# Transposing x from the fifth block on: 32x32 squares on VectorE and DMAs within SBUF in place of TensorE

## The chip, the cores and the metric

The kernel runs on one core of a Trainium2 chip. The metric is the device time of one execution in microseconds (us). The engines are called as the profile calls them: PE (TensorE; PEld is its weight load), DVE (VectorE), ACT (ScalarE), POOL (GpSimd) and SP (SyncE, which here only issues DMAs). A "q" behind an engine's name is its queue of instructions that issue DMAs or wait.

## The reference

The input x has 8 x 1024 tokens of 256 channels, fp32. A linear-attention layer with 16 heads of 16 channels is followed by a feed-forward layer with ternary weights; each is added to its input and normalised.

```python
q, k, v = x @ Wq.T + bq, x @ Wk.T + bk, x @ Wv.T + bv      # split into 16 heads
q = softmax(q, axis=-1)                                    # over the 16 channels of a head
k = softmax(k, axis=-2)                                    # over the 1024 tokens of a batch
out = einsum('bhnd,bhde->bhne', q, einsum('bhnd,bhne->bhde', k, v))
x = layernorm(x + (layernorm(out) * ln_g + ln_b) @ Wo.T + bo)
h = gelu((layernorm(x) * ln1_g + ln1_b) @ ternary(w1).T + b1)
x = layernorm(x + (layernorm(h) * ln2_g + ln2_b) @ ternary(w2).T + b2)
```

## The kernel before

The 8192 tokens are cut into 16 blocks of 512, two to a batch. A block's x is one SBUF tile of 128 partitions x 4 x 256: partition p holds four of the block's tokens (t = 0 to 3). For the projections x is needed with channels on partitions: xT is a tile of 128 x 2 x 512, one half of 128 channels for each k, with the 512 tokens in its columns. `turn_x` makes it. For each k, `turned` has PE transpose four squares of 128x128 into one PSUM bank (L341, the tile ptx) and ACT copies the bank to xT (L342). `turned` also turns the queries after their softmax (`turn_queries`, the tile ptq, copied to qT).

From xT, `queries` computes q (PE at L408, tile pq, stationary xT; DVE adds the bias at L412) with tokens on partitions, and `keys` computes the keys (PE at L362, tile pk) with channels on partitions and tokens in columns. `keys_exp` takes their exponential on ACT, with the sum over the tokens (L382, to ekT). `turn_keys` turns ekT back to tokens on partitions (PE at L395, ACT at L399), and `keys_x` multiplies with x (PE at L451, tile pa). `attend` applies the state of a whole batch to qT (PE at L546, tile po; ACT copies at L551 and L552; DVE's statistics sto at L556). `turn_input` turns the normalised input of the feed-forward layer (PE L633, ACT L637 and DVE L638 make the upper and the lower half of hT). `hidden` (PE L661, tile ph; ACT L667, L670, L651), `lower` (DVE L688, tile u) and `product` (PE L733, tile pf) are the feed-forward layer. `rest` closes a block on DVE (L805, L810, L814, L816). `finish` scales it on POOL (L847), stores it from SP (L850) and then loads the block nine further on into the same x tile (L77). The reductions of squares are DMAs on POOL's queue that accumulate within SBUF (sums from sq, L696; sums from sums, L704); two more add constant rows to x (L619 and L1000).

The order of the work is written out by hand. Each engine runs its instructions in the order of the program. The table ORDER has one string of pieces per slot: slots 0 to 3 use "early", slots 4 to 15 "mid", and five more close the work. In slot i the queries and keys of block i are computed, x of block i+1 is turned (tx0 and tx1, one for each k), and the feed-forward layer of a block some slots back runs in pieces (H, A, B). `m4` and the like pull steps of `rest` and of the norms from a list. In "mid", tx0 and tx1 stand 18 pieces apart, with the turned queries, two or three pieces of `attend` and the turned keys between them, and the first reader of the turned x is q0 of the next slot:

```python
"mid": """
    H m6 H m q0 q2 m1 m2 m3 m st0/tp qm m6 H st1/tp sq/w H p m k0 p k1 p kb p m3 H H A m8
    A A st2/w m1 H A tq0/tp H m3 A st3/w A ke p tx0 A bs m m4 m2 a/ph A m4 m a/w tq1/ph
    a/w te0 p B te2/w be qe p tx1/w p B B m1 en B bw qs x0 ti1/ph p m4 m a/w x1 m4 B cr
    m1 m3 ti0/ph B m2 m3 B m m2 p p B sh
"""
```

SP's queue holds the loads of the weights and of the first nine blocks at the start, and after that only one store and one load per finished block, 43 DMAs in all. Of the DMAs from SP and ACT, each waits in the built program for the one eight before it.

Of the kernel before, what the change touches and what calls it, by code (L numbers as in the profile page):

```python
# [8 lines left out]
F32 = mybir.dt.float32  # L9
I32 = mybir.dt.int32  # L10
F32R = mybir.dt.float32r
AF = mybir.ActivationFunctionType
# [3 lines left out]
P = 128  # L16
EPS = 1e-5
XBUFS = 9
BANKS = {"tp": 1, "w": 3, "ph": 2, "pf": 2}
LAG = 6  # L20
RING = 10
ROUND = 12582912.0

# [2 lines left out]
def attn_ffn_postln_kernel(  # L26
# [11 lines left out]
    nc = tc.nc  # L38
    B, N, C = x.shape
# [3 lines left out]
    KC = C // P  # L43
    HC = HID // P
    NT = N // P
    G = 4
# [3 lines left out]
    const = ctx.enter_context(tc.tile_pool(name="const", bufs=1))  # L50
    xpool = ctx.enter_context(tc.tile_pool(name="xpool", bufs=XBUFS))
    small = ctx.enter_context(tc.tile_pool(name="small", bufs=4))
    big = ctx.enter_context(tc.tile_pool(name="big", bufs=1))
# [1 line left out]


    wqkv_sb = const.tile([P, KC, 3 * C], F32, name="wqkv_sb")
    wo_sb = const.tile([P, KC, C], F32, name="wo_sb")

    t1 = const.tile([P, KC, HID], F32R, name="t1")  # L60

# [75 lines left out]
    def power(v, name):  # L137
# [5 lines left out]
        nc.gpsimd.tensor_tensor(y, v, mhalf[:, :n], ALU.pow)  # L143
        yield LAG
        nc.vector.tensor_tensor(t, y, y, ALU.mult)
# [15 lines left out]
    w1s, w2s = (  # L161
        [big.tile([P, 2 * TB], F32, tag="u", bufs=RING, name=f"{name}_{i}") for i in range(2)]
        for name in ("w1", "w2")
# [14 lines left out]
    def quantise(parts, t_sb, inv, name):  # L178
        part = small.tile([P, 2], F32, tag="part", name=f"part_{name}")
        for i, w in enumerate(parts):  # L180
            yield
            size = big.tile([P, 2 * TB], F32, tag="u", bufs=RING, name=f"size_{name}_{i}")
            nc.scalar.activation(size, w, AF.Abs, accum_out=part[:, i : i + 1])
# [26 lines left out]
    def rows_of(w, vecs, n, m, name):  # L210
# [3 lines left out]
        for j in range(n):  # L214
            nc.tensor.matmul(pr[:rows, :C], vecs(j), w(j), start=(j == 0), stop=(j == n - 1))
        row = big.tile([P, TB], F32, tag="u", bufs=RING, name=f"row_{name}")[:rows, :C]
        nc.vector.tensor_copy(row, pr[:rows, :C])
# [9 lines left out]
    def prepare1():  # L227
# [5 lines left out]
        nc.vector.tensor_scalar(gs1, ln1_g, inv1, None, ALU.mult)  # L233
        row = big.tile([P, 2 * TB], F32, tag="u", bufs=RING, name="row_1")[:2, :]
        for c in range(0, HID, TB):
# [85 lines left out]
    xT, q, qT, ekT, ek, pa = {}, {}, {}, {}, {}, {}  # L321
    es, mb, z, mx, a0, aT, sT, sm = {}, {}, {}, {}, {}, {}, {}, {}
    ys, mvo = {}, {}

    def x_of(i):
        return xs[i]
# [7 lines left out]
    def bank(name):  # L334
        return bank_of([P, TB], name)

    def turned(dst, src, k, name):

        pt = bank(name)
        for t in range(G):  # L340
            nc.tensor.transpose(pt[:, t * P : (t + 1) * P], src[:, t, k * P : (k + 1) * P], ident)  # L341
        nc.scalar.copy(dst, pt)  # L342

    def turn_x(i, k):
        if i >= len(blocks):
            return
        if k == 0:
            xT[i] = big.tile([P, KC, TB], F32, tag="xT", bufs=2, name=f"xT_{i}")
        turned(xT[i][:, k, :], x_of(i), k, f"ptx_{i}_{k}")

    def keys(i, c):

# [24 lines left out]
    def keys_exp(i):  # L377

        b, g = blocks[i]
        dst = big.tile([P, KC, TB], F32, tag="ekT", name=f"ekT_{i}")  # L380
        for c in range(KC):
            nc.scalar.activation(  # L382
                dst[:, c, :], ekT[i][c], AF.Exp, bias=mx[i][:, c : c + 1],
                accum_out=z[b][:, g, c : c + 1],
            )
        ekT[i] = dst

# [51 lines left out]
    def turn_queries(i, k):  # L439
        if not 0 <= i < len(blocks):  # L440
            return
        if k == 0:
            qT[i] = big.tile([P, KC, TB], F32, tag="qT", bufs=2, name=f"qT_{i}")
        turned(qT[i][:, k, :], q[i], k, f"ptq_{i}_{k}")

    def keys_x(i, c):

# [205 lines left out]
    def hidden(n):  # L653
# [13 lines left out]
        nc.scalar.activation(ph[n], ph[n], AF.Gelu, bias=bh[:, j : j + 1])  # L667
        u[n] = big.tile([P, 2, TB], F32R, tag="u", bufs=RING, name=f"u_{n}")
        if not upper_on_vector(n):
# [28 lines left out]
    def upper_on_vector(n):  # L698

        return len(blocks) - 4 < n // HC < len(blocks) - 1 and n % 3 == 1  # L700
# [244 lines left out]
    def piece(what, i):  # L945
# [33 lines left out]
        elif what == "kb" and real:  # L979
            keys_bias(i)  # L980
        elif what == "ke" and real:
            keys_exp(i)
        elif what == "bs" and real and g == 1:
            blocks_sum(b)
# [8 lines left out]
        elif what == "cr" and real:  # L993
# [8 lines left out]
            )  # L1002
        elif what in ("tx0", "tx1"):
            turn_x(i + 1, int(what[2]))
        elif what[:2] == "tq" and i > 0:
            one = turn("tq", NBL, KC)
            if one:
                turn_queries(*one)
# [37 lines left out]
        elif what == "sq" and i > 4:  # L1046
            one = turn("sq", NBL)
            if one:
# [3 lines left out]
                if n < NBL - 1:  # L1052
                    assert count["B"] >= (n + 1) * HC
                    behind.append([rest(n, (0, G)), 0])

    turn_x(0, 0)
    turn_x(0, 1)
    for i in range(last + 5):
        names = {last + k: str(16 + k) for k in range(5)}
        for what in ORDER[names.get(i, "early" if i < 4 else "mid")].split():  # L1060
            what, _, tag = what.partition("/")
# [48 lines left out]
```

## Time and profile before

| | |
|---|---|
| median of 3 runs | 669.87 us (665.34 to 671.02) |
| profiled execution | 667.08 us, of which the span of its instructions is 665.4 us |
| granted TensorE clock, mean | 0.974 |
| transposes of x (ptx) | 128 on PE; 32 copies to xT on ACT |
| DMA packets, bytes | 33889, 64.73 MB |
| share of 16 DMA engines: POOL's queue, SP's and ACT's queue | 39.8%, 7.9% |

The profile gives for each engine its busy time as a share of the span. The chain that ended last follows the work back from the last instruction, at each step to what released it, and divides the span among the engines and lines it passes. A group is all instructions of one line, operation and pair of tiles, with its busy time and the idle time just before them. A timeline row gives start, duration, engine, line, operation and tiles. A DMA row gives the time from its issue to its landing. The slots 6 to 14, from 190 to 521 us, take 36 to 37 us each; the tx0 and tx1 of the twelve blocks from the fifth on lie in slots 3 to 14. A slot is called odd or even by its number.

### The profile page before, as it was taken

The page shows a single profiled execution, that of the slowest core. Times are in us where ns is not written, and L with a number is a line of the kernel's source. Part 1 is how long each engine was busy: PE and PEld are TensorE (multiplying, and loading weights), DVE is VectorE, ACT ScalarE, POOL GpSimd, SP SyncE. Part 2 cuts the span into 40 slices and gives each one's busy share as a digit, 9 for nine tenths or more (in the row PEclk, how much of TensorE's full clock was granted, in tenths as well). Part 3 has the DMA queues.
Part 4 walks back from the last instruction along what each step waited for, and adds up shares of the span by engine and source line. Part 5 has one row for each costly group of instructions (what it writes and reads, how often), then busy time and mean ns, then how long its engine had stood idle before and what let it go on. Part 6 is the DMA issues. An engine that isn't in the chain of part 4 may idle for free.

```text
span 665.4 us, 9546 instructions
## 1 busy us (share of the span) xinstructions
PE 605.4 (91%) x3200; PEld 478.2 (72%) x3200; DVE 511.3 (77%) x1448; ACT 498.3 (75%) x939; POOL 338.6 (51%) x315
## 2 busy tenths in 40 slices
PE   5799989999999999999999999999999989778850
PEld 3467657878787787868787887878787777566750
DVE  1666776388877797888978887888878888867886
ACT  2554388798897979787887979797979887758720
POOL 1123453545464645646455646456464644765461
PEclk9999999999999999999999999999999999978875
DMA  8522232545365563637463755635354644372321
GB/s 289 208 33 33 32 49 47 96 80 96 48 159 80 115 122 83 129 67 151 80 149 59 159 79 119 120 82 103 61 121 75 125 75 107 56 119 70 89 63 64
DMA packets 33889, 64.73 MB, mean 97 GB/s; under 512 B 3344, under 2 KB 21776, under 8 KB 33840
## 3 DMA queue, kind: packets, MB, share of 16 engines
q0 software_dynamic: 25328, 43.92, 39.8%
q1 hardware_dynamic: 8240, 19.94, 7.9%
q8 instruction: 25, 0.41, 0.3%
q10 hardware_dynamic: 272, 0.26, 0.1%
q14 instruction: 24, 0.20, 0.1%
HBM read 11.95 MB, written 8.39 MB: 31 GB/s over the span
## 4 chain that ended last, share of the span: by engine, by line
PE 64%; DVE 12%; ACT 10%; DMA 4%; issue 4%; POOL 4%; SPq 1%; POOLq 0%; DVEq 0%
PE ph L661 13%; PE pf L733 11%; PE po L546 9%; PE pk L362 8%; PE pa L451 7%; PE pq L408 6%; DVE u L688 3%; ACT sq L651 2%; ACT ph L667 2%; DMA sums<-sums 2%; PE pth L633 2%; PE ptq L341 1%; PE pte L395 1%; PE ptx L341 1%; DVE x L805 1%
## 5 line engine op out<-in xcount | busy, mean ns | idle before, releaser
L733 PE MATMUL pf<-t,u 128*128 128x258 f32 x1024 | 164.0, 300 | 2.3 <-DVE u L688 1.3
L661 PE MATMUL ph<-hT,t 128*128 128x512 f32 x512 | 149.7, 423 | 13.3 <-DVE u L688 10.0
L733 PEld LDWEIGHTS pf<-t,u 128*128 128x128 f32 x1024 | 141.7, 194 | 14.9 <-DVE u L688 4.1
L688 DVE SCALAR_TENSOR_TENSOR u<-ph,gm,u 128x512 fp32r<-128x512 f32 x128 | 95.3, 748 | 51.8 <-ACT sq L651 47.2
L661 PEld LDWEIGHTS ph<-hT,t 128*128 128x128 f32 x512 | 92.0, 192 | 41.0 <-DVE u L688 16.7
L667 ACT ACTIVATE ph<-ph,bh 128x512 f32<-128x512 f32 x128 | 85.1, 665 | 24.1 <-PE ph L661 23.3
L546 PE MATMUL po<-sm,qT 128*128 128x384 f32 x256 | 93.0, 488 | 0.0
L670 ACT ACTIVATE u<-ph,gm 128x512 fp32r<-128x512 f32 x123 | 84.7, 689 | 4.0
L696 POOL DMA_DIRECT2D sums<-sq x45 | 41.5, 923 | 58.3 <-DMA sums<-sq 17.4
L616 POOL TENSOR_SCALAR h<-x,rs_all 128x256 f32<-128x256 f32 x64 | 64.6, 1208 | 7.2 <-ACT x L894 6.2
L651 ACT ACTIVATE sq<-ph,shift 128x512 f32<-128x512 f32 x96 | 65.4, 682 | 0.1
L143 POOL TENSOR_TENSOR ny_y<-nvy,mhalf 128x8 f32<-128x8 f32 x16 | 27.1, 1696 | 74.7 <-DVE nvy L585 74.7
L435 POOL TENSOR_TENSOR q<-q,rq 128x1024 f32<-128x1024 f32 x16 | 31.4, 1962 | 61.2 <-DVE rq L434 59.1
L451 PE MATMUL pa<-x,ek 128*128 128x256 f32 x256 | 60.6, 380 | 0.2 <-ACT ek L399 0.2
L408 PE MATMUL pq<-wqkv_sb,xT 128*128 128x256 f32 x256 | 58.8, 382 | 0.0
L362 PE MATMUL pk<-xT,wqkv_sb 128*128 128x512 f32 x128 | 58.0, 593 | 0.4 <-DVE q L412 0.4
L546 PEld LDWEIGHTS po<-sm,qT 128*128 128x128 f32 x256 | 43.8, 190 | 20.2 <-ACT sm L533 3.0
L422 POOL TENSOR_TENSOR q<-q,qm 128x1024 f32<-128x1024 f32 x16 | 30.9, 1933 | 52.2 <-DVE qm L421 50.1
L451 PEld LDWEIGHTS pa<-x,ek 128*128 128x128 f32 x256 | 47.4, 190 | 9.5 <-ACT ek L399 0.9
L408 PEld LDWEIGHTS pq<-wqkv_sb,xT 128*128 128x128 f32 x256 | 48.5, 191 | 8.0 <-issue 1.2
L637 ACT ACTIVATE hT<-pth,gs 128x512 fp32r<-128x512 f32 x32 | 21.9, 688 | 33.3 <-PE pth L633 33.3
L143 POOL TENSOR_TENSOR ny_f<-nv_f,mhalf 128x8 f32<-128x8 f32 (+2 forms) x17 | 26.6, 1563 | 30.5 <-DVE nv_f L780 30.4
(171 smaller groups left out, 1149.1 us busy)
## 6 DMA issues: line engine op xcount, KB each, us to landing
sums<-sq POOLq DMA_DIRECT2D x45, 512.0 KB, 4.6
x<-in_x_dram SPq DMA_DIRECT2D x16, 512.0 KB, 6.6
x<-crow POOLq DMA_DIRECT2D x16, 512.0 KB, 5.5
x<-bout POOLq DMA_DIRECT2D x16, 512.0 KB, 5.5
out_dram<-x SPq DMA_DIRECT2D x15, 512.0 KB, 2.7
sums<-sums POOLq DMA_DIRECT2D x13, 256.0 KB, 6.1
w<-in_w_dram SPq DMA_DIRECT2D x4, 512.0 KB, 8.0
wqkv_sb<-in_wqkv_dram SPq DMA_DIRECT2D x2, 256.0 KB, 6.7
```

The source lines that it names most:

```text
L143: nc.gpsimd.tensor_tensor(y, v, mhalf[:, :n], ALU.pow)
L362: nc.tensor.matmul(pk, wqkv_sb[:, k, C + c * P : C + (c + 1) * P], xT[i][:, k, :], start=(k == 0), stop=(k == KC - 1),)
L408: nc.tensor.matmul(pq[:, n, :], xT[i][:, k, (t + n) * P : (t + n + 1) * P], wqkv_sb[:, k, 0:C], start=(k == 0), stop=(k == KC - 1),)
L451: nc.tensor.matmul(pa[i][:, c, :], ek[i][:, t, c * P : (c + 1) * P], x_of(i)[:, t, :], start=(t == 0), stop=(t == G - 1),)
L546: nc.tensor.matmul(po[:, c * P : c * P + P + C], qT[i][:, c, t * P : (t + 1) * P], sm[b][:, c, :], start=(c == 0), stop=(c == KC - 1), ski ...
L616: nc.gpsimd.tensor_scalar(h0[i][:, t, :], x_of(i)[:, t, :], rs2[:, t : t + 1], None, ALU.mult)
L651: nc.scalar.activation(sqs[n], ph[n], AF.Square, bias=shift)
L661: nc.tensor.matmul(ph[n], t1[:, k, j * P : (j + 1) * P], hT[i][s][:, k, :], start=(s == 0 and k == 0), stop=(s == 1 and k == KC - 1),)
L667: nc.scalar.activation(ph[n], ph[n], AF.Gelu, bias=bh[:, j : j + 1])
L670: nc.scalar.activation(u[n][:, 0, :], ph[n], AF.Copy, scale=gm[:, j : j + 1])
L688: nc.vector.scalar_tensor_tensor(u[n][:, 1, :], ph[n], gm[:, j : j + 1], u[n][:, 0, :].bitcast(F32), ALU.mult, ALU.subtract,)
L733: nc.tensor.matmul(pf[i, m][t], u[n][:, s, (2 * m + t) * P : (2 * m + t + 1) * P], t2[:, j, :], start=(j == 0 and s == 0), stop=(j == HC - ...
```

## The change

Blocks 0 to 3 are turned as before. For blocks 4 to 15, `turn_x` calls a new function, `turned_by_dma`. One VectorE instruction transposes all the 32x32 squares of a 128 x 512 half in place of their own, into a tile of 128 x 4 x 128 (tag "sx", one buffer). Then 16 DMAs from SP, each of 32 partitions x 128 columns, bring each group of squares to the partitions it belongs on. The columns of such an xT stand in another order: first by quarter of the partitions, then t, then the partition within the quarter. The copy to qT and the exponential to ekT put them back in the old order by the pattern in which they read or write. `wo_sb`, which is read only at the start, shares the buffer of the new tile.

```diff
+W = 32
+SQ = P // W
+BY_DMA = 4
...
-    wo_sb = const.tile([P, KC, C], F32, name="wo_sb")
+    wo_sb = big.tile([P, KC, C], F32, tag="sx", name="wo_sb")
...
-    def turned(dst, src, k, name):
+    def turned(dst, src, k, name, of_quarters=False):
 
         pt = bank(name)
         for t in range(G):
             nc.tensor.transpose(pt[:, t * P : (t + 1) * P], src[:, t, k * P : (k + 1) * P], ident)
+        if of_quarters:
+            dst, pt = by_tiles(dst), by_quarters(pt)
         nc.scalar.copy(dst, pt)
+
+    def turned_by_dma(dst, src, k, name):
+
+        squares = big.tile([P, SQ, P], F32, tag="sx", name=name)
+        nc.vector.transpose(
+            squares.rearrange("p b (t j) -> p t b j", t=G),
+            src[:, :, k * P : (k + 1) * P].rearrange("p t (b i) -> p t b i", b=SQ),
+        )
+        for a in range(SQ):
+            for b in range(SQ):
+                nc.sync.dma_start(
+                    dst[b * W : (b + 1) * W, k, a * P : (a + 1) * P],
+                    squares[a * W : (a + 1) * W, b, :],
+                )
...
-        turned(xT[i][:, k, :], x_of(i), k, f"ptx_{i}_{k}")
+        if i < BY_DMA:
+            turned(xT[i][:, k, :], x_of(i), k, f"ptx_{i}_{k}")
+        else:
+            turned_by_dma(xT[i], x_of(i), k, f"sx_{i}_{k}")
+
+    def by_quarters(v):
+        return v.rearrange("p (a t j) -> p a t j", a=SQ, t=G)
+
+    def by_tiles(v):
+        return v.rearrange("p (t a j) -> p a t j", a=SQ, t=G)
...
+            to, of = dst[:, c, :], ekT[i][c]
+            if i >= BY_DMA:
+                to, of = by_tiles(to), by_quarters(of)
             nc.scalar.activation(
-                dst[:, c, :], ekT[i][c], AF.Exp, bias=mx[i][:, c : c + 1],
-                accum_out=z[b][:, g, c : c + 1],
+                to, of, AF.Exp, bias=mx[i][:, c : c + 1], accum_out=z[b][:, g, c : c + 1]
             )
...
-        turned(qT[i][:, k, :], q[i], k, f"ptq_{i}_{k}")
+        turned(qT[i][:, k, :], q[i], k, f"ptq_{i}_{k}", i >= BY_DMA)
```

## The prediction

> **What bounds the kernel now.** I read the page first: busy shares, then the chain that ended last, then the groups, then the table of DMA issues.
>
> ```profile
> span 665.4 us, 9546 instructions
> ...
> PE 605.4 (91%) x3200; PEld 478.2 (72%) x3200; DVE 511.3 (77%) x1448; ACT 498.3 (75%) x939; POOL 338.6 (51%) x315
> ...
> PE 64%; DVE 12%; ACT 10%; DMA 4%; issue 4%; POOL 4%; SPq 1%; POOLq 0%; DVEq 0%
> ```
>
> TensorE (PE) is busy 91% of the span and holds 64% of the chain, so work taken from PE looks like time won. Next, the tile of the removed work (the PSUM tile ptx), then the chain in a stretch of one slot of the hand-written order, 224 to 262 us:
>
> ```profile
> L341 PE MATMUL ptx<-ident,x x128: 271/273/476, 5.7 to 491.1; 128*128 128x128 f32 x128
> L342 ACT COPY xT<-ptx x32: 565/586/701, 6.9 to 492.7; 128x512 f32<-128x512 f32 x32
> ...
> 226.38 0.44 PE ptx L341 x4
> ...
> 233.75 0.44 PE ptx L341 x4
> ...
> 243.14 1.86 PE ph L661 x8
> 245.01 3.45 PE pq L408 x16
> ```
>
> Four transposes hold the chain for 0.44 us. Between the second group of a block and its first reader (pq of the next block) lie 11 us of other PE work. Now what the replacement shares: SyncE's queue (SP), from its timeline, and the landing times.
>
> ```profile
> 227.75 0.34 SPq L850 DMA_DIRECT2D out_dram<-x  x1
> 230.46 0.33 SPq L77 DMA_DIRECT2D x<-in_x_dram  x1
> ...
> sums<-sq POOLq DMA_DIRECT2D x21, 512.0 KB, 4.6
> out_dram<-x SPq DMA_DIRECT2D x7, 512.0 KB, 2.7
> x<-in_x_dram SPq DMA_DIRECT2D x7, 512.0 KB, 5.8
> ```
>
> The last three are of the stretch 180 to 420 us: KB each, and median us from issue to landing. A DMA that starts on SP costs SP a third of a microsecond and lands no sooner than 2.6 us (2.7 median; least 2.6). Last, VectorE (DVE) at the two places where the new transposes are put, from its timeline:
>
> ```profile
> 229.51 0.49 DVE L810 SCALAR_TENSOR_TENSOR x<-g2sum,ms,x 128x256 f32<-128x256 f32 x1
> 229.92 0.16 DVE L459 TENSOR_TENSOR m<-mb 128x2 f32<-128x2 f32 x1
> ...
> 235.70 0.15 DVE L816 BATCH_NORM_AGGREGATE mvf<-st_f 128x2 f32<-128x6 f32 x1
> 235.77 0.39 DVE L556 BATCH_NORM_STATS2 sto<-o 128x6 f32<-128x256 f32 x1
> ```
>
> In the built order the first new transpose stands between the first two of these, the second between the last two: 5.9 us apart, and DVE is not idle in between.
>
> **Removed.** 12 blocks x 2 tiles = 24 groups of four transposes, 24 x 0.44 = 10.6 us of PE, and 24 copies of 0.59 = 14 us of ACT. Both lie between the first transpose and pq, the stretch that the new chain below lengthens, so I credit nothing: PE and ACT will wait there anyway. If the new chain were short, the credit would be at most the 10.6.
>
> **Added on DVE.** 24 transposes of 128x512. No row shows the operation; rows of that size run from 424 ns (TENSOR_SCALAR, L201) to 748 (L688). I take 0.70, by the reductions and additions that touch each element once (684 at L366, 683 at L412). The Trainium skill, "VectorE: DVE Perf Modes", section The three transpose paths, gives 311 ns for 128x128 in bf16; four of them would be an estimate of 1.24 us, and a slot, with two on its chain, would come out 1.1 us longer, 737 in all instead of 725. No run here shows which yet.
>
> **Added on SP.** 16 DMAs of 32 rows x 512 B (16 KB) per tile, 384 in all, in a queue that had 43. Three prices.
> - Spacing: SP rows last 0.33 to 0.35 mid-run and stood 0.39 to 0.50 apart at the start (6.15 to 6.54; 1.69 to 2.19). Take 0.40; ends 0.33 and 0.50.
> - Landing: no row moves 16 KB within SBUF from SP. Nearest by queue is the store, least 2.6 (2.3 for its 256 KB form); nearest by path are the accumulating DMAs of GpSimd's queue, 4.6 (sums from sq) and 6.1 (sums from sums). I take 2.6, since a plain copy on SP is nearer to the store; ends 2.3 and 6.1.
> - Depth: in the built program each SP DMA waits for the one eight before it, so the ninth starts 3.2 us after the first or when the first has landed.
>
> A tile then takes 15 x 0.40 + 2.6 = 8.6 us. The Trainium skill, "DMA: Bandwidth & Descriptors", section Anatomy of one DMA, fits 2.0 us + bytes/436e3 for DMAs of the GpSimd path, an estimate of 2.04 for 16 KB; with it a tile is 8.0 us and the sum about 713. Its section Rules for kernel authors wants many small transfers made into one large one, which speaks against this change.
>
> **What is queued ahead.** Seven tiles (blocks 7 to 13) stand in SP's order behind a store and a load of 512 KB. The store waits for GpSimd's L847, which ends at 227.72, 2.3 us before the first transpose point, and is gone in time: SP is free at 230.46 + 0.33 = 230.8 when DVE's first transpose ends, 230.0 + 0.7 = 230.7. The load was issued just ahead and lands after 5.8 us, and I take it that small DMAs behind it on the queue land after it. The row for that is the start, where cols_sb, 12 KB behind 1.3 MB on SP, took 7.4 us. So the ninth DMA starts only when the load is in.
>
> **The new wait on DVE.** Both transposes of a block write one buffer, so the second waits on DVE for all 16 DMAs of the first. Queued behind it stand sto (norm of the attention), rq (GpSimd's L435 waits for it) and hT's lower half, for which PE's ph waits. pq waits for the second tile.
>
> **The sum, slot by slot,** against the old times:
> - Odd slot with load: first DMA 230.8, load in at 236.3, ninth at 236.4, sixteenth 239.2, landed 241.8; second transpose to 242.5; DMAs 242.6 + 8.6 = 251.2. pq was at 244.8: +6.4. DVE is 242.5 - 235.85 = 6.6 late, less 0.5 of idle before hT: about the same.
> - Even slot with load (store 191.22, load 194.30, transpose points 193.54 and 198.38, pq 208.81): ninth 200.2, landed 205.6, transpose to 206.3, 206.4 + 8.6 = 215.0: +6.2. DVE's 7.9 loses 4 us of old idle, so it is not the later one.
> - Odd without load: 230.8 + 8.6 = 239.4, 240.1, 240.2 + 8.6 = 248.8: +4.0. Even without: +3.5. Slot 4 (transpose point 119.26, pq 135.76): 138.05, +2.3. Slot 3: its points lie 10.7 us apart and pq 12 us further on: 0.
>
> Sum: 0 + 2.3 + 4.0 (block 6) + 4 x 6.2 + 3 x 6.4 + 4.0 (block 14) + 3.5 (block 15) = 57.8 us. From pq to the next first transpose the order is as before, and every engine arrives late by about the same, so nothing is won back. The profiled run took 667.08 us (span 665.4), 2.8 under the median of 669.87; 667.1 + 57.8 = 725. The copies that now read or write PSUM columns out of order I cost at nothing: L551, which steps over columns of po, takes 0.39 beside 0.40 for its dense neighbour L552. At worst they cost 0.12 each, as far as xT's copies spread above their median (586 to 701 ns); with four a block that is 0.5 us of ACT, half of what the removed copies give back.
>
> **Rivals.**
> 1. *The small DMAs land late* because GpSimd's accumulating DMAs fill the engines (DMA share 0.76 in 226 to 231 us, 0.61 in 233 to 245). With the 4.6 of sums from sq, a tile is 4.6 + 2.8 + 4.6 = 12.0; odd slots cost 10.8 (11.8 with load), even 10.3 (11.6), slot 4 9.1, slot 3 2.7: 125 us, 793. Against: the store's 2.6 us, which moves 32 times the bytes in the same stretch.
> 2. *The load does not hold the small ones up.* Then the seven cost 3.5 or 4.0: 667.1 + 57.8 - 18 = 707. For: cols_sb's 7.4 us could be the crowd at the start.
> 3. *Not slower: the DMAs fit under the old work.* Both tiles must take under (244.84 - 230.8 - 0.8)/2 = 6.6 us, for which, with 2.6 to land, DMAs must follow at 0.27 us or less; 32 rows instead of 128 could do that. DVE then still waits until a tile takes 5.1. The prize is at most 11 x 0.88 = 10 us: 657 to 667. Against: no SP row under 0.327.
>
> **How the numbers follow.** Forecast as summed, 705 to 750 with both prices a little off: 0.45. Rival 1 (750 to 800): 0.23. Rival 2 and cheaper prices (683 to 705; 0.33 spacing, 2.3 landing and no hold-up give 683): 0.20. Rival 3: 0.07. Above 800 (landing towards 6.1, which gives about 850): 0.05. The range 685 to 795 takes in all but about 0.15. This measurement can tell about 1% from no change: faster 0.04, same 0.04 (rival 3, with a little of rival 2), slower 0.92.
>
> **What would show it.** Right: DVE's second transpose idle some 3 to 6 us on SP's DMAs; PE's pq as long a wait on DMA; small DMAs about 0.4 apart, landing in 2 to 3 us, those behind a load in 5; blocks 7 to 13 costlier than 6 and 14; PE's share down towards 83%. Wrong: pq without a wait; the first eight DMAs behind a load landing as soon as others; a transpose far from 0.7; ACT or GpSimd the engine that pq or ph waits for.

## The result and the profile after

The changed kernel takes 795.87 us (median of 4 runs, 793.41 to 800.11); the kernel before took 668.12 beside it. The ratio is 1.192 (95% interval 1.187 to 1.196): 19% slower, 0.9 us above the range that was predicted. The profiled execution took 800.11 us with a span of 798.3. From one store to the next, a slot took 36.6 us before (191.22 to 447.51 in seven slots) and takes 48.4 now (217.74 to 605.02 in eight): 11.8 us more, in eleven slots.

The page of the changed kernel: busy shares, the chain, and the group of the new transposes.

```profile
span 798.3 us, 9985 instructions
...
PE 639.1 (80%) x3104; PEld 489.4 (61%) x3104; DVE 528.3 (66%) x1472; ACT 486.4 (61%) x915; POOL 341.9 (43%) x315
...
SPq 31%; PE 22%; ACT 14%; DVE 13%; DMA 9%; issue 7%; POOL 4%; DVEq 0%; POOLq 0%; ACTq 0%
...
L353 DVE STREAM_TRANSPOSE sx<-x 128x512 f32<-128x512 f32 x24 | 16.9, 706 | 106.4 <-DMA xT<-sx 106.4
...
xT<-sx SPq DMA_DIRECT2D x384, 16.0 KB, 1.8
```

PE's 64% of the chain has become 22%, and SP's queue, which held 1%, holds 31%: not waiting, but issuing. DVE stood 106 us before the second transposes. The DMAs themselves land in 1.8 us in the median. The chain through the first tile of one slot (start us, us, what) shows where the time is spent:

```profile
269.81 0.86 SPq L359
...
272.84 0.59 SPq L359
273.43 0.04 issue
273.47 0.59 SPq L359
274.06 0.04 issue
274.10 0.59 SPq L359
...
275.37 1.94 SPq L359
277.31 0.04 issue
277.35 0.90 SPq L359
...
281.46 1.76 DMA xT<-sx
...
283.35 0.71 DVE sx L353
```

Most DMAs hold SP for 0.59 us, and these follow at 0.635. Some hold it for 0.9 to 1.9 us. From the first issue (269.59) to the last landing (283.2) the tile takes 13.6 us. PE's timeline of that slot, with the idle time and its releaser in brackets, shows what the second half of the slot waits for:

```profile
287.70 1.65 PE L694 MATMUL ph<-hT,t 128*128 128x512 f32 x3 [6.29 <-DVE hT L671]
291.22 2.50 PE L694 MATMUL ph<-hT,t 128*128 128x512 f32 x5 [1.88 <-DVE hT L671]
293.51 4.39 PE L441 MATMUL pq<-wqkv_sb,xT 128*128 128x256 f32 x14
298.19 0.67 PE L441 MATMUL pq<-wqkv_sb,xT 128*128 128x256 f32 x2 [0.29 <-DMA xT<-sx]
```

PE waits 8 us for hT's lower half, which stood behind DVE's wait. pq starts before the second tile is in: its sixteen matmuls take the tokens by quarters of xT, so only the last two wait for the last DMAs. They do so for each of the twelve blocks, for 0.1 to 1.9 us.

### The profile page after: what moved, and what is told of

Same layout as the page of the kernel before. It is cut to its first block, busy times and chain, and to the rows that moved or that the text cites. A ratio compares the mean times of both kernels' runs of the same rounds, so it can differ in the third digit from the quotient of the medians.

```text
span 798.3 us, 9985 instructions
## 1 busy us (share of the span) xinstructions
PE 639.1 (80%) x3104; PEld 489.4 (61%) x3104; DVE 528.3 (66%) x1472; ACT 486.4 (61%) x915; POOL 341.9 (43%) x315
## 4 chain that ended last, share of the span: by engine, by line
SPq 31%; PE 22%; ACT 14%; DVE 13%; DMA 9%; issue 7%; POOL 4%; DVEq 0%; POOLq 0%; ACTq 0%
SPq L359 31%; DMA xT<-sx 7%; PE ph L694 5%; ACT sq L684 5%; ACT ph L700 4%; PE pk L393 4%; PE po L579 3%; PE pq L441 3%; DVE u L721 3%; DMA x<-in_x_dram 2%; ACT u L703 2%; PE pf L766 2%; ACT x L927 2%; DVE x L838 1%; DVE sx L353 1%
## 5 line engine op out<-in xcount | busy, mean ns | idle before, releaser
L694 PE MATMUL ph<-hT,t 128*128 128x512 f32 x512 | 174.2, 474 | 99.2 <-DVE hT L671 91.3
L694 PEld LDWEIGHTS ph<-hT,t 128*128 128x128 f32 x512 | 102.9, 217 | 137.7 <-DVE hT L671 103.0
L766 PE MATMUL pf<-t,u 128*128 128x258 f32 x1024 | 162.3, 299 | 4.4 <-DVE u L721 2.8
L353 DVE STREAM_TRANSPOSE sx<-x 128x512 f32<-128x512 f32 x24 | 16.9, 706 | 106.4 <-DMA xT<-sx 106.4
L441 PE MATMUL pq<-wqkv_sb,xT 128*128 128x256 f32 x256 | 75.5, 448 | 9.9 <-DMA xT<-sx 9.8
L441 PEld LDWEIGHTS pq<-wqkv_sb,xT 128*128 128x128 f32 x256 | 58.2, 234 | 27.7 <-issue 12.8
L649 POOL TENSOR_SCALAR h<-x,rs_all 128x256 f32<-128x256 f32 x64 | 66.6, 1331 | 7.2 <-ACT x L927 6.2
```

The source lines that it names most:

```text
L441: nc.tensor.matmul(pq[:, n, :], xT[i][:, k, (t + n) * P : (t + n + 1) * P], wqkv_sb[:, k, 0:C], start=(k == 0), stop=(k == KC - 1),)
L649: nc.gpsimd.tensor_scalar(h0[i][:, t, :], x_of(i)[:, t, :], rs2[:, t : t + 1], None, ALU.mult)
L694: nc.tensor.matmul(ph[n], t1[:, k, j * P : (j + 1) * P], hT[i][s][:, k, :], start=(s == 0 and k == 0), stop=(s == 1 and k == KC - 1),)
L766: nc.tensor.matmul(pf[i, m][t], u[n][:, s, (2 * m + t) * P : (2 * m + t + 1) * P], t2[:, j, :], start=(j == 0 and s == 0), stop=(j == HC - ...
```

## The experiments

Theory S: SP's queue is the pace; 32 DMAs go through it one after the other in each slot. Rivals: W, that DVE's wait at the head of its order is the cost; C, that the new bytes crowd with GpSimd's DMAs. The kernel before ran beside each batch at 667.8 to 669.1 us.

**1. A buffer for each half.**

```diff
-        squares = big.tile([P, SQ, P], F32, tag="sx", name=name)
+        squares = big.tile([P, SQ, P], F32, tag=("sx", "aT")[k], name=name)
```

> The squares of the second half get a buffer of their own (that of aT, which is free then), so VectorE's second transpose no longer waits for the first tile's 16 DMAs. Theory S (SP's queue is the pace: 32 DMAs in series, some 0.635 us each, behind the store and the load): the wait only moves from hT to pq. SP saves the landing of the first tile and one transpose in each slot, about 2.5 us: 765 to 778. Theory W (the wait at the head of VectorE's order is the cost, 106 of the 128 us): it goes, 690 to 700.

775.45 us (770.3 to 785.1 in four executions), ratio 1.159 (1.151 to 1.167). DVE no longer waits, and the wait stands on PE. The waits of the profiled execution, the longest of the four (engine, line, what for: us in total, times, longest):

```profile
PE pq L441 <- DMA xT<-sx: 72.7, 32, 5.4
...
PEld pq L441 <- DMA xT<-sx: 23.5, 8, 5.8
```

Some 20 us of 128 are won, as S says. W falls as the cause: the wait on DVE is only where SP's pace is first felt.

**2. Four wide DMAs to a tile.**

```diff
-        for a in range(SQ):
-            for b in range(SQ):
-                nc.sync.dma_start(
-                    dst[b * W : (b + 1) * W, k, a * P : (a + 1) * P],
-                    squares[a * W : (a + 1) * W, b, :],
-                )
+        for b in range(SQ):
+            nc.sync.dma_start(dst[:, k, b * P : (b + 1) * P], squares[:, b, :])
```

> Each tile goes in 4 DMAs of 128 partitions x 128 columns, the same bytes and rows in a quarter of the instructions; the squares stay on their own partitions, so xT is not the transpose of x and the values of the output are others. Theory S: a tile takes 4 x 0.635 + 1.8 = 4.3 us and both are in before pq: 660 to 685. Theory C (the bytes and rows crowd with GpSimd's accumulating DMAs): little changes, above 760. If one such DMA holds SP 0.35 us as the store does, the price of 0.59 belongs to the shape of 32 rows; if 0.59, to both ends lying in SBUF or to the short rows.

681.3 us, ratio 1.022 (1.017 to 1.028). With the same bytes in a quarter of the instructions, 115 us of the 128 are gone, so C's bytes by themselves are not the cause. A shorter wait of DVE for the first tile is left (16.6 us in all, nine times). One such DMA holds SP 0.607 us in the median: with 128 rows about as long as with 32 (0.589).

**3. One half of x alone.**

```diff
...
-        if i < BY_DMA:
-            turned(xT[i][:, k, :], x_of(i), k, f"ptx_{i}_{k}")
+        if i < BY_DMA or k == 1:
+            turned(xT[i][:, k, :], x_of(i), k, f"ptx_{i}_{k}", "to" if i >= BY_DMA else False)
```

(with "to", `turned` writes xT in the new order of columns)

> Only the first half of each block's x (k = 0) goes over VectorE and SP; the second half is transposed by TensorE as before, with its columns in the new order. Theory S: 16 DMAs, 13.6 us with the hold-up by the load, start 14 us before pq needs them: nearly all hidden, 668 to 685, not half of the 128 us. Theory W: the same place, since nothing waits on VectorE: 668 to 685. Theory C or any cost that goes with the number of DMAs: half, about 732.

670.41 us, ratio 1.005 (1.002 to 1.008). Half of the DMAs cost nearly nothing: PE comes to pq some 14 us after the first of them and waits 3.0 us for them in the whole run. The cost does not go with the number of DMAs, but with what goes over the 14 us.

**4. The turns earlier in the slot.**

```diff
-            H m6 H m q0 q2 m1 m2 m3 m st0/tp qm m6 H st1/tp sq/w H p m k0 p k1 p kb p m3 H H A m8
+            H m6 H m q0 q2 tx0 m1 m2 m3 m st0/tp qm m6 H st1/tp sq/w H p m k0 p k1 p kb p tx1 m3 H H A m8
```

(and both taken out of their old places, with a buffer for each half as in the first experiment)

> In the slots from the fifth on, the two turns of x stand earlier: the first behind q2, the second behind kb, each with its own buffer of squares; all else as in the changed kernel. From the first transpose to pq there are then 30 us and more in place of 15. Theory S: 32 DMAs need about 27 us and fit; the 10.6 us of TensorE and 14 us of ScalarE that were taken away count for the first time, against 17 us more of VectorE: 655 to 680. Theory C: the DMAs slow the accumulating ones wherever they stand: above 700.

672.95 us, ratio 1.008 (1.005 to 1.011). All 384 DMAs are there, nothing waits for them, and 123 of the 128 us are gone. But the 10.6 us of PE that were taken away do not show. The chain of this run points to the reason:

```profile
PE 35%; DVE 31%; ACT 17%; POOL 6%; issue 6%; DMA 5%; DVEq 0%; SPq 0%; POOLq 0%
```

DVE, 12% of the chain before, now holds about as much as PE. Experiment 8 leaves its transposes out.

**5. What holds SP.**

```diff
+    for n in range(8):
+        nc.sync.dma_start(there[0:32, n * 128 : n * 128 + 128], here[32:64, 0:128])
+    for n in range(8):
+        nc.sync.dma_start(there[:, n * 128 : n * 128 + 128], here[:, 0:128])
+    for n in range(8):
+        nc.sync.dma_start(there[32:64, n * 128 : n * 128 + 128], x[0][32:64, 0:128])
+    for n in range(4):
+        nc.sync.dma_start(there[32 * n : 32 * n + 32, 0:1024], here[32 * n : 32 * n + 32, 0:1024])
+    for n in range(2):
+        nc.sync.dma_start(there[:, 0:1024], here[:, 0:1024])
```

> The changed kernel with five kinds of DMA put on SP at the start, where its queue is idle (behind the loads, from about 17 us), between a scratch tile, another and x in HBM; nothing reads what they write. Asked is how long SP is held by each. If the 0.59 us belongs to both ends lying in SBUF, all but the kind from HBM take 0.59 and that takes 0.35. If it belongs to rows of 512 B, the kinds with rows of 4 KB take 0.35. If it belongs to few partitions, the kinds of 128 take 0.35; the wide form of the second experiment (0.607 at 128 partitions) speaks against that.

The rows of the five lines, in that order (ns least/median/most, first and last start in us):

```profile
L184 SPq DMA_DIRECT2D price<-price x8: 507/508/597, 17.5 to 26.9; - x8
```

```profile
L186 SPq DMA_DIRECT2D price<-price x8: 592/599/608, 27.4 to 32.0; - x8
```

```profile
L188 SPq DMA_DIRECT2D price<-in_x_dram x8: 419/514/1917, 32.6 to 38.9; - x8
```

```profile
L190 SPq DMA_DIRECT2D price<-price x4: 507/572/589, 39.4 to 41.5; - x4
```

```profile
L192 SPq DMA_DIRECT2D price<-price x2: 508/510/511, 43.9 to 47.9; - x2
```

None of the three readings holds as I put it. Neither the length of the rows nor their number matters. Within SBUF a DMA holds SP 0.51 when it stands apart (the first eight start 1.3 to 1.5 us apart, since each waits for an earlier load to land, and all but one take 0.51; the last two start 4 us apart), and 0.56 to 0.61 when it follows another at once. Of the eight from HBM five take 0.42 to 0.44 and the others 0.59 to 1.9, against 0.34 for the lone loads of the slots. A load or a store costs more right behind the small DMAs, too: 0.58 for the load in the next experiment, 0.52 for the store in the fourth. So two things make up the 0.25 us between 0.34 and 0.59: both ends in SBUF (0.51 against 0.34 for a lone 512 KB), and standing in a row. They do not simply add, and how they divide the 0.25 us in a row is not settled.

**6. The load behind the tiles.**

```diff
...
+        if k == 1:
+            while loads:
+                load(loads.pop(0))
...
-        load(i + XBUFS)
+        loads.append(i + XBUFS)
```

> The load that follows a block's store is put behind the 32 DMAs of the slot in SP's order. If the load holds up the small DMAs behind it (their first lands 5 to 6 us after its issue, and the ninth starts some 2 us late), seven slots get 2 to 2.5 us shorter, and SP no longer waits for the store to land before the first tile (another 1 to 2.7 us): 770 to 783. If the small ones are slow for another reason: 790 to 800.

790.16 us, ratio 1.185 (1.180 to 1.190), beside 1.192 for the change. The load costs at most some 6 us in seven slots, under 1 us each, not 2.4. The order on the queue is real: in the changed kernel the first small DMA behind a load lands 4.8 to 6.2 us after its issue, at once after the load. But at 0.635 the ninth DMA starts 8 x 0.635 = 5.1 us after the first, when the load is nearly in (5.3 us to land in that stretch).

**7. VectorE's transposes alone, in the kernel before.**

```diff
         turned(xT[i][:, k, :], x_of(i), k, f"ptx_{i}_{k}")
+        if i >= 4:
+            squares = big.tile([P, 4, P], F32, tag="sx", name=f"sx_{i}_{k}")
+            nc.vector.transpose(
+                squares.rearrange("p b (t j) -> p t b j", t=G),
+                x_of(i)[:, :, k * P : (k + 1) * P].rearrange("p t (b i) -> p t b i", b=4),
+            )
```

(with `wo_sb` in the buffer of the new tile, as in the change)

> The kernel before, with the 24 VectorE transposes added at the places where the change has them; their result is not used, and TensorE transposes as before. If VectorE's 17 us lie on the path (it held 31% of the chain when the turns stood early): 674 to 682. If they fall into its waits for ScalarE: 667 to 671.

667.44 us, ratio 0.999 (0.997 to 1.001): 17 us more of DVE cost nothing in the kernel before, whose chain is mostly PE's.

**8. The early form without VectorE.**

```diff
-                    squares[a * W : (a + 1) * W, b, :],
+                    src[a * W : (a + 1) * W, b, k * P : (k + 1) * P],
```

(in the form of experiment 4, with the transpose left out)

> As the early form, but the 16 DMAs of a tile read x itself (32 rows x 512 B, the same count and size) and VectorE's transposes are left out; xT is then not the transpose and the output's values are others. It shows what is left of taking 10.6 us of TensorE and 14 us of ScalarE away when neither VectorE nor a wait pays for it. If the path follows TensorE: 655 to 662. If the DMAs cost something by crowding with GpSimd's: 666 to 673, as the early form.

662.54 us, ratio 0.992 (0.989 to 0.995): half a microsecond above the first of the two ranges, clear of the second. PE holds most of the chain again:

```profile
PE 60%; DVE 15%; ACT 15%; issue 4%; POOL 3%; DMA 1%; SPq 0%; ACTq 0%; POOLq 0%
```

Taking PE's transposes and ACT's copies away is worth 0.8%, 5 us, when DVE does not pay for it. With all 384 DMAs in, this run is some 9 us shorter than the fourth, each against its kernel before, so it is DVE's transposes, and what waits for them, that used the gain up there. Of the 10.6 us of PE half is still missing, and the runs do not say whether the DMAs take it.

**9. Two blocks ahead.**

```diff
-BY_DMA = 4
+BY_DMA = 6
...
-            H m6 H m q0 q2 m1 m2 m3 m st0/tp qm m6 H st1/tp sq/w H p m k0 p k1 p kb p m3 H H A m8
+            H m6 H m q0 q2 m1 m2 m3 m st0/tp qm m6 H st1/tp sq/w H p m k0 p k1 p kb p m3 ty0 H H A m8
...
-            a/w te0 p B te2/w be qe p tx1/w p B B m1 en B bw qs x0 ti1/ph p m4 m a/w x1 m4 B cr
+            a/w te0 p B te2/w be qe p tx1/w ty1 p B B m1 en B bw qs x0 ti1/ph p m4 m a/w x1 m4 B cr
...
         elif what in ("tx0", "tx1"):
-            turn_x(i + 1, int(what[2]))
+            if i + 1 < BY_DMA:
+                turn_x(i + 1, int(what[2]))
+        elif what in ("ty0", "ty1"):
+            if i + 2 >= BY_DMA:
+                turn_x(i + 2, int(what[2]))
```

> x is turned two blocks ahead, into the buffer that the slot's own queries and keys have just left, for blocks 6 to 15 (4 and 5 by TensorE as before). The first transpose stands where VectorE waited for ScalarE's squares (some 14.8 us before the second), the second where the change has it. Theory S, with 13.6 us for a tile: neither VectorE nor pq waits, and with VectorE's transposes at places that cost nothing (the run with them alone) the time is that of the early form without VectorE: 660 to 666, under the kernel before. If the DMAs cost something by themselves wherever they stand: 668 to 675.

670.29 us, ratio 1.003 (1.000 to 1.005). The waits are gone but for 8.3 us on DVE, of which 3.9 in one slot, and the gain does not come: S's 660 to 666 is missed, and the time lies in the range that I gave to DMAs that cost something wherever they stand. The run before speaks against that reading, since there the DMAs stood early, too, and the time was 662.54. DVE holds the most of the chain in this run:

```profile
DVE 38%; PE 27%; ACT 13%; POOL 7%; issue 5%; SPq 5%; DMA 4%; DVEq 0%; POOLq 0%; ACTq 0%
```

So the run with VectorE's transposes alone misled me: they were free while PE was late anyway. That they lie on the path once PE is relieved is what the fourth and the eighth run show; for this order it is only read from the chain. No version of this change that transposes x and that I ran beats the kernel before.

**10 and 11. Without GpSimd's accumulating DMAs,** in the changed kernel and in the kernel before. The four `nc.gpsimd.dma_start(..., accum_op=ALU.add)` are left out in both, one of them shown:

```diff
-                nc.gpsimd.dma_start(sums[i], sq[i], accum_op=ALU.add)
+                pass
```

> The changed kernel without GpSimd's accumulating DMAs (the constant rows added to x and the sums of squares are left out, so the output's values are others). If it is these DMAs that stretch some of SP's issues from 0.59 to 1.3 us and more, a tile takes 15 x 0.635 + 1.8 = 11.3 us instead of 13.6, and the distance to the kernel before, both without them, falls from 128 us to about 104. If not, it stays at 120 to 130.

> The kernel before without the same DMAs, as the measure for the run with the change: 655 to 668, since its chain holds them at 4%.

753.59 and 664.81 us: the distance is 89 us, not 128, and 15 less than the 104 that I expected. In the changed kernel without them, the 32 DMAs of a slot take SP 22.0 to 23.5 us, DVE's wait within included, in place of 26.4 to 27.7. In the run with them, the stretches in which SP's issues are long are those in which the DMA engines are full. The stretches of the changed kernel, whose next to last column is the DMA share (over 1 where packets overlap), and the chain in the last of them:

```profile
269.50:275.00 5.50, 5.50 (x37) 4.77 (x36) 4.60 (x17) 4.62 (x13) 4.64 (x5) 1.00 0.81 185
275.20:278.30 3.10, 3.10 (x16) 2.35 (x15) 0.00 (x0) 1.33 (x3) 0.00 (x0) 1.00 1.11 168
286.00:292.00 6.00, 2.43 (x5) 1.52 (x6) 5.42 (x14) 2.69 (x5) 4.66 (x4) 0.50 0.11 25
292.00:295.00 3.00, 3.00 (x9) 2.35 (x8) 2.83 (x9) 2.89 (x5) 0.54 (x1) 0.50 1.08 158
...
292.24 1.32 SPq L359
293.60 1.40 SPq L359
295.04 3.01 DMA xT<-sx
```

In the second and the fourth the chain has issues of 0.9 to 1.9 us, in the third only 0.59. Over the whole run 78 of the 384 hold SP longer than 0.7 us, 68 of them where the share, taken over the 0.6 us from the issue's start, is over 1; without GpSimd's DMAs 8 do. So these DMAs cost the change about 39 us, mostly by holding SP longer: from its first issue to its last a tile takes 11.7 us on average in place of 9.7. Late landings are the smaller part: the last DMA of a tile lands in 1.8 us, but in 3.0 to 3.3 in six of the 24 tiles. For this part of the cost rival C holds.

## Why the prediction was right or wrong

**The sign, the two waits and their places: right.** The second transpose waits for the first tile on DVE, hT's lower half behind it makes PE wait, and nothing is won back before the next slot. The credit of nothing for the 10.6 us of PE held too; even the early form, in which nothing waits for the DMAs, does not keep it.

**The step that failed: the spacing of SP's DMAs,** taken as 0.40 with ends of 0.33 and 0.50; it is 0.635, outside both. The rows nearest to a run of DMAs were in the trace of the kernel before, at the start (start us, us):

```profile
0.80 0.37 SPq L77 DMA_DIRECT2D x<-in_x_dram  x1
1.22 0.42 SPq L86 DMA_DIRECT2D wqkv_sb<-in_wqkv_dram  x1
1.69 0.46 SPq L77 DMA_DIRECT2D x<-in_x_dram  x1
2.19 0.43 SPq L89 DMA_DIRECT2D cols_sb<-in_cols_dram  x1
2.67 0.50 SPq L90 DMA_DIRECT2D wo_sb<-in_wo_dram  x1
3.21 0.54 SPq L91 DMA_DIRECT2D wqkv_sb<-in_wqkv_dram  x1
3.80 0.61 SPq L77 DMA_DIRECT2D x<-in_x_dram  x1
```

These seven start 0.42 to 0.59 us apart, 0.50 in the mean, so the prediction's "0.39 to 0.50" left out the two longest. I took the lone stores and loads of the slots for the duration and a value near the shortest spacing at the start. A run of 16 is priced by rows of a run; they would have given 0.50 to 0.59, and no DMA that SP issues in the kernel before has both ends in SBUF. A tile without crowding is then 15 x 0.635 + 1.8 = 11.3 us, not 8.6. The 0.235 us more in 15 spacings are 3.5 us a tile, 7 a slot and some 78 in eleven slots: alone more than the 71 us by which the sum fell short. The long issues add to it; the shorter landing, the smaller hold-up and pq's early start take off.

**The landing: too long,** 2.6 against 1.8 in the median. The estimate of 2.04 from the Trainium skill, "DMA: Bandwidth & Descriptors", section Anatomy of one DMA, came nearer, though its fit is for the GpSimd path. With it the sum is 12 us lower (713) and so further from the 796 that were measured: it was not the landing that counted most.

**Rival 1: the right number by the wrong mechanism.** It gave 793 with landings of 4.6 us. GpSimd's DMAs do make a tile longer, 13.6 us, but mostly as issues of 0.9 to 1.9 us on SP; the landings stayed at 1.8 in the median. That its 793 lies within 3 us of the result is luck: it left the spacing at 0.40.

**The hold-up by the load: too large,** 2.4 us in the sum and under 1 in the run with the load moved. At the predicted 0.40 the ninth DMA would have been ready after 3.2 us and stood until the load was in; at 0.635 it is ready when the load has nearly landed. So the sign "blocks 7 to 13 costlier than 6 and 14" did not come either: from the end of one pq to the next, in the profiled executions, these seven slots got 10.5 to 12.6 us longer, those of blocks 6 and 14 11.8 and 12.1.

**pq as one wait: wrong by 3 us the other way.** Fourteen of its sixteen matmuls (3.0 of 3.45 us) run before the last quarter is in. With 13.6 us a tile and this, an odd slot gives 230.8 + 13.6 + 0.8 + 13.6 - 3.0 = 255.8 against 244.8, 11.0 us, an even one 194.3 + 13.6 + 0.8 + 13.6 - 3.0 = 219.3 against 208.8, 10.5. Eleven such slots make 118 us; in the profiled executions they got 127.6 longer, from pq to pq. Slot 3, which the prediction put at nothing, cost 2.9. Where the other 10 us are is open.

**VectorE's 0.70 us: right** (0.706). The estimate of 1.24 from the Trainium skill, "VectorE: DVE Perf Modes", section The three transpose paths, did not hold for this form: 0.706 for four squares of 128x128 in fp32 is 177 ns each, where the page gives 311 for one in bf16.

## What to carry to other kernels

When work moves to DMAs, count the instructions on the issuing queue before the bytes: a tile in many small DMAs costs their number times the queue's spacing, read from rows that stand in a run, and the landing only once. Then ask what the first reader's distance is and put the whole series under it: half of the DMAs, or all of them earlier, cost under 1% here, where all of them in 15 us cost 19%. And relief of the bounding engine that is paid for on the next busiest one has to be tried with both; an added operation that is free before the relief need not be free after it. Sharing the issues between two engines' queues, the obvious next step, was not tried here.

## What the runs showed of the hardware

- A DMA between two places in SBUF holds SP 0.51 us alone (16 KB and 512 KB) and 0.56 to 0.61 in a run (16 to 128 KB); a store or load of 512 KB alone holds it 0.33 to 0.35, and 0.52 and 0.58 right behind the small DMAs.
- With the DMA engines full (share over 1) most issues of a 16 KB DMA take 0.9 to 1.9 us, up to 2.3.
- PE's granted clock falls to half for 10.2 us in nearly every slot of the changed kernel, around the 6 us in which PE waits for hT: 0.50 from 286 to 295 us in the rows above. The mean falls from 0.974 to 0.903, and ph takes 474 ns in place of 423. In that slot the clock fell at 285.7 us, 4.3 after PE's last matmul had ended (281.4), and came back at 295.9, 4.7 after the end of PE's next wait (291.2).
- The Trainium skill, "TensorE: Matmul & The Clock Gate", Part 1: The HAM clock gate, has the clock halved after about 3.4 us of idling and given back after about 3.4 us of sustained work. Both stretches here are somewhat longer.
- What the halved clock costs in time was not tried by itself. It is back before the last two matmuls of pq in each of these slots, and these still had to wait for the DMAs, so up to there it cost nothing; what it did to the work behind ph is open.
